# Attention scores of a macaron block: two of four query tiles computed as whole tiles, the last tile with its sides exchanged

## The chip, the cores and the metric

The kernel runs on one core of a Trainium2 chip. The core has a matrix engine (TensorE, "PE" in the profile, with its weight loads as "PEld"), a vector engine (VectorE, "DVE"), a scalar engine (ScalarE, "ACT"), a general engine (GpSimd, "POOL") and a queue that issues transfers (SyncE, "SP"). The metric is the device time of one execution in microseconds; lower is better. Everything is float32.

## The reference

A block of three parts is applied to `x` of shape (16, 512, 256): half a feed-forward part, attention, half a feed-forward part again, each added to `x`. The change touches attention alone:

```python
q = x @ Wq + bq                                   # x: the normalized input, (16, 512, 256)
k, v = jnp.split(x @ Wkv + bkv, [H * DQK], axis=-1)
q, k = _rope(heads(q)), _rope(heads(k))           # 16 heads of 64
scores = jnp.einsum('bhqd,bhkd->bhqk', q, k) * (1.0 / np.sqrt(DQK))
scores = jnp.where(causal, scores, -jnp.inf)      # a query sees keys up to its own place
probs = jax.nn.softmax(scores, axis=-1)
out = jnp.einsum('bhqk,bhkd->bhqd', probs, v)
return out.reshape(b, s, H * DV) @ Wo + bo
```

## The kernel before

Attention is worked off in 64 units, one for each batch (16) and group of four heads (4). A unit has 512 queries in four tiles of 128, numbered 0 to 3; by causality tile `i` needs `(i+1)*128` keys. The order of PE, DVE, ACT, POOL and SP in attention is written out by hand in the loop over `u` (from -2 to 63): each engine does its instructions in the order in which that loop gives them.

**Scores** (`Weights.scores`, L1038 to L1058). A head's 64 dimensions lie as two halves of 32 (the two parts of the rotation), the four heads of a unit in four groups of 32 rows. So a score matmul contracts 32 rows, is done for `n` = 0, 1 and accumulated, and the four heads stand beside each other in the four row groups of the array; each head has a PSUM bank of its own (`banks[j]`). Each tile is split into two halves of 64 queries, which stand on the two halves of the array's columns. The 64 early queries of a tile need 64 keys fewer than the late ones, so one half streams `w - 64` columns and the other `w`. Which half of the columns has the early queries alternates with the tile: in tiles 3 and 1 the first half, in tiles 2 and 0 the second. The 64 columns that the early half doesn't write are filled with zeros by a small bf16 matmul of a blank tile (L1047). Tiles 3 and 2 have four banks each (`scores((3,))`, `scores((2,))`); tiles 1 and 0 share four (`scores((1, 0))`).

An f32 matmul shows in the trace as two records of PE, each with a weight load of its own.

**Softmax** (`exps`, L1061 to L1079). For each head and tile DVE adds the causal mask, scales and takes the smallest (L1073), and ACT takes the exponential with its sum (L1077). `mask(i)` (L905) picks blocks of 128 columns out of one constant, `causal`, of 128 x 640, which POOL fills once. Since the sides alternate, there are two diagonal masks: one in the last block, for tiles with an even number, and one in block 3, for the odd ones.

**Weights onto values.** The weights are divided by their sums on POOL (L1085), turned in squares of 32 on DVE (L1100) and moved by SP (L1127). `sums` (L1149 to L1170) multiplies them with the values into `p_av` (L1158), and ACT copies the result out (L1169), adds the bias, and puts the queries of tiles whose sides are exchanged back in order: one copy for the odd tiles, two for the even ones. `leave` (L1171) multiplies with `Wo` into `p_ay` (L1176) and DVE adds it onto `x` (L1182).

**Order.** In a middle iteration PE does: `p_av` of unit `u`, scores of tiles 3 and 2 of unit `u+2`, `p_ay` of `u`, queries and keys of `u+3` (`p_q`, `p_k`, L988), values of `u+1` (`p_v`, L1010), scores of tiles 1 and 0 of `u+2`. PSUM has 8 banks in rotation: `p_ay` takes the bank that the scores of tile 3, head 0, had, and `p_av` those of the two key halves.

## Time and profile before

| | |
|---|---|
| median of 3 runs | 2297.73 us (2296.9 to 2299.47) |
| the profiled execution's own time | 2299.21 us |
| its span | 2297.5 us |
| attention, by the scores' first and last record | 410 to 1888 us of the span |
| score passes (L1054) | 8192, 303.4 us in which at least one runs |
| blank passes (L1047) | 1024 |
| distance of one attention unit from the next, in the middle | 23.26 us |
| granted clock of TensorE | 1.00 in the stretches shown below |

How to read what is shown below: in a group's line stand the line of the code, engine, operation, the tiles written and read, shapes and count, then the time in which at least one of them ran and the mean of one in ns, then the idle time of the engine just before them and who ended it. `32*64` in front of a matmul's shape is the part of the array that it uses, rows by columns. In the view by order of time a line has the start in us from the span's start, the length in us, and then the same; equal neighbours are put together, and records of two kinds that run side by side alternate, so that the shape is that of the first. Matmuls are pipelined: the end of a record is modelled, and the starts of two neighbours are the better measure. In the table of stretches each engine has its busy time and, in brackets, its number of instructions. In the waits stand who waited, for whom, the total in us, how often, and the longest.

### The profile page before, as it was taken

The page shows a single profiled execution, that of the slowest core. Times are in us where ns is not written, and L with a number is a line of the kernel's source. Part 1 is how long each engine was busy: PE and PEld are TensorE (multiplying, and loading weights), DVE is VectorE, ACT ScalarE, POOL GpSimd, SP SyncE. Part 2 cuts the span into 40 slices and gives each one's busy share as a digit, 9 for nine tenths or more (in the row PEclk, how much of TensorE's full clock was granted, in tenths as well). Part 3 has the DMA queues.
Part 4 walks back from the last instruction along what each step waited for, and adds up shares of the span by engine and source line. Part 5 has one row for each costly group of instructions (what it writes and reads, how often), then busy time and mean ns, then how long its engine had stood idle before and what let it go on. Part 6 is the DMA issues. An engine that isn't in the chain of part 4 may idle for free. (4 is left out here: it accounts for less than half of the span.)

```text
span 2297.5 us, 52884 instructions
## 1 busy us (share of the span) xinstructions
PE 2242.8 (98%) x19544; PEld 1486.4 (65%) x19544; DVE 1764.4 (77%) x4678; ACT 1158.7 (50%) x3296; POOL 1068.9 (47%) x1695
## 2 busy tenths in 40 slices
PE   7999999999999999999999999999999999998999
PEld 4664488566666666666666666666666666764588
DVE  6742298789989898989898989989888875432387
ACT  5743243555555555556465546555555565532233
POOL 2210053565566566565655565656556552210053
PEclk9999999999999999999999999999999999999999
DMA  6839851044545364454554554536455443839834
GB/s 223 251 123 404 334 141 56 12 129 122 141 116 159 100 157 125 127 136 113 146 133 126 131 144 108 159 96 162 120 132 131 124 117 113 239 137 406 309 118 139
DMA packets 221929, 359.52 MB, mean 156 GB/s; under 512 B 99876, under 2 KB 159848, under 8 KB 213480
## 3 DMA queue, kind: packets, MB, share of 16 engines
q1 hardware_dynamic: 220812, 355.34, 52.4%
q8 instruction: 155, 2.54, 0.5%
q14 instruction: 102, 0.84, 0.1%
q10 hardware_dynamic: 860, 0.81, 0.1%
HBM read 156.29 MB, written 37.22 MB: 84 GB/s over the span
## 5 line engine op out<-in xcount | busy, mean ns | idle before, releaser
L1085 POOL TENSOR_SCALAR pr<-pr,ars 128x512 f32<-128x512 f32 (+3 forms) x1024 | 524.1, 532 | 566.7 <-DVE ars L1082 565.5
L1077 ACT ACTIVATE pr<-pr,amn 128x512 f32<-128x512 f32 (+3 forms) x1024 | 561.8, 550 | 211.5 <-DVE amn L1073 207.1
L1100 DVE STREAM_TRANSPOSE sq<-pr 128x768 f32<-128x768 f32 x434 | 384.6, 918 | 79.6 <-DMA prT<-sq 56.8
L1073 DVE CUSTOM_DVE_ANT_0 pr<-p_as,causal 128x512 f32<-128x512 f32 (+2 forms) x768 | 309.4, 459 | 46.3 <-PE p_as L1054 46.1
L1054 PE MATMUL p_as<-k,q 32*64 32x448 f32 (+3 forms) x8192 | 303.4, 412 | 0.0
L1013 ACT COPY v<-p_v 128x512 f32<-128x512 f32 x128 | 74.8, 586 | 449.9 <-PE p_v L1010 449.9
L1158 PE MATMUL p_av<-prT,v 128*64 128x512 f32 (+3 forms) x2048 | 289.8, 435 | 9.3 <-ACT pr L1077 1.6
L1158 PEld LDWEIGHTS p_av<-prT,v 128*64 128x64 f32 x2048 | 160.3, 137 | 138.0 <-issue 93.1
L1176 PE MATMUL p_ay<-wo,aoT 128*128 128x256 f32 x1024 | 238.5, 386 | 0.8 <-ACT aoT L1169 0.5
L1054 PEld LDWEIGHTS p_as<-k,q 32*64 32x64 f32 x8192 | 206.6, 131 | 46.1 <-issue 23.7
L1010 PE MATMUL p_v<-wv,ahT 128*128 128x256 f32 x1024 | 231.6, 379 | 0.7 <-DVE x L1182 0.7
L988 PE MATMUL p_q<-ahT,wq 128*128 128x512 f32 x512 | 230.6, 593 | 0.2 <-ACT ahT L949 0.2
L988 PE MATMUL p_k<-ahT,wk 128*128 128x512 f32 x512 | 230.3, 592 | 0.0
L1010 PEld LDWEIGHTS p_v<-wv,ahT 128*128 128x128 f32 x1024 | 194.5, 190 | 53.8 <-issue 23.2
L1176 PEld LDWEIGHTS p_ay<-wo,aoT 128*128 128x128 f32 x1024 | 189.1, 190 | 55.8 <-DVE amn L1073 31.7
L1077 ACT ACTIVATION_READ_ACCUMULATOR pr<-pr,amn 128x1 f32 x1024 | 192.1, 188 | 0.0
L988 PEld LDWEIGHTS p_k<-ahT,wk 128*128 128x128 f32 x512 | 97.3, 190 | 122.0 <-issue 106.9
L988 PEld LDWEIGHTS p_q<-ahT,wq 128*128 128x128 f32 x512 | 97.0, 190 | 95.7 <-issue 78.4
L1073 DVE CUSTOM_DVE_ANT_1 pr<-p_as,causal 128x384 f32<-128x384 f32 x256 | 130.2, 546 | 0.0
L1169 ACT ACTIVATE aoT<-p_av,bcol 128x128 f32<-128x128 f32 (+1 forms) x384 | 117.4, 392 | 7.8 <-PE p_av L1158 7.8
L811 PE MATMUL p_cy<-vw,catT 128*128 128x256 f32 x512 | 120.8, 379 | 0.0
L584 PE MATMUL p_ds<-hT,qk 128*128 128x512 f32 x256 | 116.2, 597 | 2.1 <-ACT hT L159 2.1
(179 smaller groups left out, 3353.7 us busy)
## 6 DMA issues: line engine op xcount, KB each, us to landing
prT<-sq SPq DMA_DIRECT2D x992, 160.0 KB
w<-in_e_W_dram SPq DMA_DIRECT2D x64, 1024.0 KB
w<-in_e_Wg_dram SPq DMA_DIRECT2D x32, 1024.0 KB
out_dram<-x SPq DMA_DIRECT2D x64, 256.0 KB
awaya<-sqa SPq DMA_DIRECT2D x25, 512.0 KB
atT<-awaya SPq DMA_DIRECT2D x100, 128.0 KB
xl<-in_attn_x_dram SPq DMA_DIRECT2D x16, 512.0 KB
xl<-out_dram SPq DMA_DIRECT2D x16, 512.0 KB
```

Source lines behind the costliest of these rows:

```text
L584: nc.tensor.matmul(psc, qk[:, k, c * P:(c + 1) * P], hT[:, k, :], start=(k == 0), stop=(k == NC - 1))
L811: nc.tensor.matmul(py[:, t * D:(t + 1) * D], atT[:, c, t * P:(t + 1) * P], vws[b][:, c, :], start=(c == 0), stop=(c == NC - 1))
L988: nc.tensor.matmul(pq, self.w[:, k, at:at + P], hTs[self.b][:, k, :], start=(k == 0), stop=(k == NC - 1))
L1010: nc.tensor.matmul(pv[:, t * 256:(t + 1) * 256], hTs[b][:, k, (t0 + t) * P:(t0 + t + 1) * P], wv[:, k, hg * HG * DQ:(hg + 1) * HG * DQ], s ...
L1054: nc.tensor.matmul(banks[j][half * H:(half + 1) * H, at:at + wh], q[n][rows, q0:q0 + H], k[n][rows, :wh], start=(n == 0), stop=(n == 1))
L1073: nc.vector.tensor_tensor_reduce(out=by_block(self.at(i, j)), in0=by_block(banks[j][:, at:at + w]), in1=mask(i), scale=-1.0 / math.sqrt(DQ ...
L1077: nc.scalar.activation(self.at(i, j), self.at(i, j), AF.Exp, bias=self.mn[:, i, j:j + 1], scale=-1.0, accum_out=self.rs[:, i, j:j + 1])
L1085: nc.gpsimd.tensor_scalar(self.at(i, j), self.at(i, j), self.rs[:, i, j:j + 1], 1.0, ALU.mult, ALU.mult)
L1100: nc.vector.transpose(view(self.sq, j * blocks * SQ + dst[0] * SQ, [(blocks * SQ, nh)] + [(s * SQ, n) for s, (_, n) in zip(dst[1:], of)] + ...
L1158: nc.tensor.matmul(po[j * DQ:(j + 1) * DQ, :].rearrange("d (a f) -> d a f", a=NSQ)[:, :, t * SQ:], vs[u][:, t, head * DQ:(head + 1) * DQ], ...
L1169: nc.scalar.activation(dst[:, odd, to], src[:, odd, of], AF.Identity, bias=bcol[:, r:r + 1])
L1176: nc.tensor.matmul(py[:, t * D:(t + 1) * D], oTs[u][:, pair, (t0 + t) * P:(t0 + t + 1) * P], wo[:, hg * (HG // 2) + pair, :], start=(pair ...
```

## The change

Tiles 1 and 0 have all 128 queries on the whole width of the array: one matmul of `w` columns for each head and `n`, without blanks. Tiles 3 and 2 stay in halves (`by_halves`), but their sides are exchanged: tile 3 has its late queries on the first half, tile 2 its early ones. So only tile 3 has its queries out of order, and the mask, the constant behind it and the copies of L1169 follow: one copy for tiles 0 to 2 of 384 columns, two of 64 columns for tile 3, in place of one of 256 and two of 128.

```diff
-        nc.gpsimd.affine_select(out=causal[:, :S], in_=causal[:, :S], compare_op=ALU.is_ge, fill=NEG, base=S - P,
-                                pattern=[[-1, S]], channel_multiplier=1)
+        nc.gpsimd.affine_select(out=causal[:, S:], in_=causal[:, S:], compare_op=ALU.is_ge, fill=NEG, base=0,
+                                pattern=[[-1, P]], channel_multiplier=1)
         for half in range(2):
-            part = causal[half * H:(half + 1) * H, S:]
+            part = causal[half * H:(half + 1) * H, S - P:S]
...
-            return by_block(causal)[:, NT - i * 2:NT + 1:2] if i % 2 == 0 else by_block(causal)[:, NT - 1 - i:NT]
+            return by_block(causal)[:, :NT] if i == NT - 1 else by_block(causal)[:, NT - i * 2:NT + 1:2]
...
                 for i in tiles:
                     w = (i + 1) * P
-                    early = slice((i + 1) % 2 * H, ((i + 1) % 2 + 1) * H)
-                    for j in range(HG):
-                        zero = blank[j * 32:(j + 1) * 32, :]
-                        nc.tensor.matmul(banks[j][early, at + w - H:at + w], zero, zero, start=True, stop=True)
-                    for n in range(2):
-                        for j in range(HG):
-                            rows = slice(j * 32, (j + 1) * 32)
-                            for half in range(2):
-                                late = half ^ (1 - i % 2)
...
+                    if i < NT // 2:
+                        for n in range(2):
+                            for j in range(HG):
+                                rows = slice(j * 32, (j + 1) * 32)
+                                nc.tensor.matmul(banks[j][:, at:at + w], q[n][rows, i * P:(i + 1) * P],
+                                                 k[n][rows, :w], start=(n == 0), stop=(n == 1))
+                    else:
+                        self.by_halves(i, q, k, banks, at)
...
+            def by_halves(self, i, q, k, banks, at):
+                w, turned = (i + 1) * P, int(i == NT - 1)
+                early = slice(turned * H, (turned + 1) * H)
+                for j in range(HG):
+                    zero = blank[j * 32:(j + 1) * 32, :]
+                    nc.tensor.matmul(banks[j][early, at + w - H:at + w], zero, zero, start=True, stop=True)
+                for n in range(2):
+                    for j in range(HG):
+                        rows = slice(j * 32, (j + 1) * 32)
+                        for half in range(2):
+                            late = half ^ turned
+                            q0, wh = i * P + late * H, w - (1 - late) * H
+                            nc.tensor.matmul(banks[j][half * H:(half + 1) * H, at:at + wh],
+                                             q[n][rows, q0:q0 + H], k[n][rows, :wh],
+                                             start=(n == 0), stop=(n == 1))
...
-            dst = oTs[u][:, pair, :].rearrange("d (i o a y) -> d o a i y", i=NT // 2, o=2, a=NSQ)
-            src = po.rearrange("d (a i o y) -> d o a i y", i=NT // 2, o=2, a=NSQ)
-            for odd, to, of in ((1, slice(0, 4), slice(0, 4)), (0, slice(2, 4), slice(0, 2)),
-                                (0, slice(0, 2), slice(2, 4))):
-                nc.scalar.activation(dst[:, odd, to], src[:, odd, of], AF.Identity, bias=bcol[:, r:r + 1])
+            dst = oTs[u][:, pair, :].rearrange("d (i a y) -> d a i y", i=NT, a=NSQ)
+            src = po.rearrange("d (a i y) -> d a i y", i=NT, a=NSQ)
+            last = slice(NT - 1, NT)
+            for to, of, tiles in ((slice(0, 4), slice(0, 4), slice(0, NT - 1)), (slice(2, 4), slice(0, 2), last),
+                                  (slice(0, 2), slice(2, 4), last)):
+                nc.scalar.activation(dst[:, to, tiles], src[:, of, tiles], AF.Identity, bias=bcol[:, r:r + 1])
```

The order of the instructions on DVE, ACT, POOL and SP is the same as before; only the shapes named above differ. On PE the scores of tiles 1 and 0 have 16 matmuls in a unit where they had 32 and 8 blank ones; the rest stands where it stood.

More of the change, by code (lines that the diff above doesn't have):

```diff
@@ L1043, in scores @@
                     w = (i + 1) * P
-                    early = slice((i + 1) % 2 * H, ((i + 1) % 2 + 1) * H)
-                    for j in range(HG):
-                        zero = blank[j * 32:(j + 1) * 32, :]
-                        nc.tensor.matmul(banks[j][early, at + w - H:at + w], zero, zero, start=True, stop=True)
-                    for n in range(2):
-                        for j in range(HG):
-                            rows = slice(j * 32, (j + 1) * 32)
-                            for half in range(2):
-                                late = half ^ (1 - i % 2)
-                                q0, wh = i * P + late * H, w - (1 - late) * H
-                                nc.tensor.matmul(banks[j][half * H:(half + 1) * H, at:at + wh],
-                                                 q[n][rows, q0:q0 + H], k[n][rows, :wh],
-                                                 start=(n == 0), stop=(n == 1))
+                    if i < NT // 2:
[6 more added lines that the diff above has]
+                        self.by_halves(i, q, k, banks, at)
                     places.append((i, at))
```

## The prediction

> **What bounds the kernel now.** I read four views in this order: the shares of busy time, the table of busy time in stretches of one attention unit, the order in time of that unit, and the waits. The profiled execution took 2299.21 us, 1.71 more than its span of 2297.5; the three runs shown have a median of 2297.73, so what I work out on the profiled execution is lowered by 1.48 to compare it with the median.

> ```profile
> PE 2242.8 (98%) x19544; PEld 1486.4 (65%) x19544; DVE 1764.4 (77%) x4678; ACT 1158.7 (50%) x3296; POOL 1068.9 (47%) x1695
> ```

> 98% on PE is an average and says nothing on who waits for whom. The change lies in attention, from 410 to about 1912 us: 64 units (a batch and four heads), all but the first two and the last with the same period, 23.26 us in the middle. Here is one of them in four stretches: scores of tiles 1 and 0; p_av; scores of tiles 3 and 2; then p_ay, q, k and v.

> ```profile
> core 0: us, PE busy (x) PEld busy (x) DVE busy (x) ACT busy (x) POOL busy (x), PEclk, DMA share, GB/s
> 1004.86:1006.72 1.86, 1.75 (x73) 1.44 (x73) 1.13 (x2) 0.59 (x1) 1.86 (x3) 1.00 1.02 367
> 1006.72:1011.18 4.46, 4.46 (x32) 2.49 (x32) 4.35 (x21) 4.09 (x18) 4.04 (x9) 1.00 0.33 57
> 1011.18:1014.25 3.07, 3.07 (x74) 1.85 (x73) 3.07 (x6) 1.27 (x5) 1.49 (x4) 1.00 0.14 21
> 1014.25:1028.22 13.97, 13.97 (x52) 9.04 (x48) 12.14 (x31) 6.03 (x17) 9.65 (x12) 1.00 0.75 196
> ```

> In the second and third stretch DVE is as full as PE (4.35 of 4.46, 3.07 of 3.07). The order in time shows how the two are tied:

> ```profile
> 1004.96 0.22 PE L1047 MATMUL p_as<-blank 32*64 32x64 bf16 x4
> 1004.98 1.17 PE L1054 MATMUL p_as<-k,q 32*64 32x256 f32 x39
> ...
> 1006.56 0.42 DVE L1073 CUSTOM_DVE_ANT_0 pr<-p_as,causal 128x256 f32<-128x256 f32 x1 [0.31 <-PE p_as L1054]
> 1006.73 4.53 PE L1158 MATMUL p_av<-prT,v 128*64 128x512 f32 x32
> ...
> 1011.18 0.22 PE L1047 MATMUL p_as<-blank 32*64 32x64 bf16 x4
> ...
> 1013.53 0.65 DVE L1073 CUSTOM_DVE_ANT_0 pr<-p_as,causal 128x512 f32<-128x512 f32 x1
> ...
> 1014.25 2.42 PE L1176 MATMUL p_ay<-wo,aoT 128*128 128x256 f32 x10
> ```

> ```profile
> PEld p_ay L1176 <- DVE amn L1073: 31.7, 62, 0.9
> PEld p_av L1158 <- issue: 93.1, 364, 0.5
> DVE pr L1073 <- PE p_as L1054: 46.1, 57, 1.7
> ```

> DVE stands idle (0.31 us here, 57 times) until the first bank of tiles 1 and 0 is signalled, at 1006.541, and starts at 1006.564. Its list of masks, reciprocals and turns then runs to 1014.207, where it frees the bank that p_ay needs; p_ay's load starts 42 ns later and its first pass at 1014.251. That is the wait of p_ay on DVE, 62 times. So the loop of one unit is: the last v pass starts at 1004.648; 1.916 us to DVE's start; 7.687 to p_ay; 13.661 of back to back passes to the next unit's last v pass; 23.264 in all. PE's own road, scores of 1 and 0, p_av, scores of 3 and 2, is a second way to the same point: its last pass (started 1013.876, 427 long) ends at 1014.303, and a new kind of tile starts 70 ns before such an end wherever nothing else holds it, so PE could have begun p_ay at 1014.233, 18 ns before it did. DVE decides, PE is close behind.

> **The change, part by part.** A pass below is one record of a matmul: an f32 matmul is two.

> *Tiles 1 and 0 whole.* Per unit, 32 score matmuls and 8 blank ones become 16: PE loses 64−32+8 = 40 passes and 40 loads. The columns go the other way: a half of the array streamed 192+128 or 256+64 = 320 columns in each of its 4 passes, the whole array streams 256+128 = 384. At 216 ns a pass of 256 (the distance of p_v's passes), 64 columns cost 54 ns, four times 0.21 us. Yet today's group isn't bound by its columns. Its row group 0 starts passes of 192 at 1005.010, .202, .365, .527, then passes of 128 at .690, .811, 1006.085 and .242: the third waits 274 ns where 107 would do, since its weights are loaded only at 1006.081. From the first blank (1004.957) to that last start are 1285 ns.

> After: the same drain of 309 ns from the last v pass. Then the first load can't hide: after a change of tile kind p_ay's first pass of 256 is 483 long against 379, so 104 ns. Then 4 × 216 for tile 1, and three steps of tile 0 to its last start. A step with 128 columns and a 128-column load is 112 ns in p_cs, 109 in the transposes:

> ```profile
> L780 PE MATMUL p_cs<-kbd,cq 128*128 128x128 f32 x256 | 33.7, 275 | 0.7 <-POOL kbd L758 0.7
> ```

> (33.7 us for 256 is 32 runs of 8 × 112 plus the end of each.) So 104 + 864 + 3 × 109 to 112 = 1295 to 1304, 10 to 19 later than now. The pass of 128 in a 32-row tile ends 267 after its start as before. The signal follows today 32 ns after that end, because the other half stands behind it; where the bank's last write also ends last (tile 2: end 1014.263, signal 1014.277) it is 14, so 18 are won back. Net −8 to +1 ns on DVE's start; I take −3: 62 units × −0.003 = −0.2 us. The price is from rows, but no row has a tile of 32 rows and 128 columns. Bounds: if the first load hid behind the drain, −104 × 62 = −6.4 us. Nothing could go at the drain itself: p_z (128 rows) to p_bcol (62 rows, same columns) at 69.0 us also starts 69 ns before the modelled end. If a pass cost its load's whole 192 ns instead of 112, 3 × 80 = +0.24 us, 62 times +14.9 us.

> [...]

> *p_av.* It starts 383 ns after the last score pass where drain alone gives 197. In front of its load PE's sequencer works off five double waits:

> ```profile
> L1158 PEldq EVENT_SEMAPHORE  x310: 51/51/4237, 470.2 to 1902.7; - x155
> ```

> Five a unit, 105 ns apart, from 1006.190 to 1006.669; the load follows at 1006.694. They stand behind the last score matmul, which is issued late today. With 64 entries instead of 144 they can be worked off under the passes: p_av gets up to 186 ns earlier, plus some 40 since the last row group's last pass moves from 1006.342 to about 1006.30. Cover: none needed, as p_ay waits for DVE anyway. This gain of up to 0.23 us goes into p_ay's wait; it is worth nothing, and up to 14.0 us (62 × 0.226) if that wait were not there. On the other side it pays for any loss in tiles 3 and 2.

> What is next: the scores of 3 and 2 would begin up to 0.23 earlier; their banks come from DVE (heads 0 and 1 of tiles 1 and 0, done by 1007.8) and, for tile 2's blanks, from ACT's second aoT group, done 1012.457, with tile 2's first pass then due at 1012.54. No wait that reaches p_ay at 1014.25.

> *Tiles 3 and 2.* The same widths change sides: each half still has 448+384 or 512+320 = 832 columns a pass set, 8 blanks stay. Issue order within a pair turns round, and the half that is ahead now comes second in it. I take 0; a stall of up to 0.2 us is under the gain of p_av.

> *Masks.* Tile 1's mask turns from one stretch of 256 into two blocks; tile 2's has always had three.

> ```profile
> L1073 DVE CUSTOM_DVE_ANT_0 pr<-p_as,causal 128x512 f32<-128x512 f32 x224 | 141.9, 669 | 0.0
> L1073 DVE CUSTOM_DVE_ANT_1 pr<-p_as,causal 128x384 f32<-128x384 f32 x224 | 114.0, 546 | 0.0
> L1073 DVE CUSTOM_DVE_ANT_0 pr<-p_as,causal 128x256 f32<-128x256 f32 x224 | 94.2, 420 | 39.7 <-PE p_as L1054 39.6
> ```

> The split 384 lies 1.5 ns above the middle of 420 and 669 (544.5). Four in a unit, +6 ns at most, +0.4 us; since the reciprocal behind them waits for ACT (114 ns), I take one of the four, +0.1.

> *ACT's aoT copies.* 256+128+128 elements become 384+64+64. Starts lie 356 and 250 apart for 256 and 128, so 106 for 128: 462 + 197 + 197 = 856, as now. If 64 cost as much as 128, +0.21 us a unit on ACT, tile 2's blanks at 1012.67, still under p_ay's wait.

> *Setup and waits.* One causal fill shrinks from 512 to 128 columns, on a POOL that then stands idle until the first q at 401.8. The waits on DVE that stood on the blanks stand on the first four whole passes; what is queued behind them is the same, and those banks are free long before.

> *Sum:* 2299.21 − 0.2 + 0.1 = 2299.1; less 1.48: **2297.6 us**.

> **Rivals.**
> *Slower: 128-column loads of a 32-row tile are not hidden.* For it: no such tile in the trace, and the load record is 192 ns against 131 for 64 columns. Against: p_cs, and four row groups loading at once today (their first passes take effect within 20 ns). DVE's start has no slack, so it decides from the first nanosecond: +14.9, 2312.5; at half the exposure 2305.
> *Faster: PE's road decides after all.* If p_ay only seems to wait for DVE, p_av's 0.226 us comes through: −14.0, 2283.6. Against it: in 11 units p_av came 28 to 182 ns late, and only there did p_ay stand at drain's distance (357 ns) from the last score pass; in the others it follows DVE's signal by 42 ns. A smaller kind is the first load hidden in the drain, −6.4, 2291.2.
> *Slower: the turned sides make tile 2 stall by more than PE's new slack,* for instance each of its four passes by 64 columns, 0.21, and its blank, 0.06: 0.05 over the cover, +3 us, 2300.7, still inside what counts as no change.

> **How the numbers follow.** A difference of 0.2%, 4.6 us or 74 ns a unit, is about what a measurement of this kernel tells from no change. No change 0.70; loads exposed 0.18, most of it above 2302.3; a way to be faster 0.12, half of it the hidden first load. The forecast's own range is 2294 to 2301. To leave out no more than 2 in 10 it takes in the hidden first load below and the half exposed load above: 2291 to 2306.

> **What would show it.** Right: period 23.26 us; DVE starts 1.91 us after the last v pass; p_av about 0.2 us after the last score pass, and p_ay's wait for DVE grown to 0.2 us; 16984 matmul records. Wrong: steps of tile 0 far from 110 ns, a DVE start that moved by over 70 ns, or p_ay no longer behind DVE.

## The result, and the profile after

The changed kernel takes 2305.46 us (median of 15 runs, 2302.01 to 2308.77); the kernel before, in as many runs beside it, 2300.52 (2296.9 to 2304.16). The ratio is 1.0021, 95% interval 1.0013 to 1.0029: slower by about 0.2%, some 5 us. The prediction was no change. The profiled execution took 2307.27 us with a span of 2305.5.

Busy time first, then one attention unit in the same four stretches as before: scores of tiles 1 and 0; p_av; scores of tiles 3 and 2; p_ay, q, k and v.

```profile
PE 2260.8 (98%) x16984; PEld 1469.8 (64%) x16984; DVE 1764.4 (77%) x4678; ACT 1158.0 (50%) x3296; POOL 1068.5 (46%) x1695
```

```profile
core 0: us, PE busy (x) PEld busy (x) DVE busy (x) ACT busy (x) POOL busy (x), PEclk, DMA share, GB/s
1009.46:1010.98 1.52, 1.52 (x33) 1.35 (x32) 0.92 (x1) 0.58 (x1) 1.52 (x2) 1.00 0.99 348
1010.98:1015.44 4.46, 4.46 (x36) 2.14 (x33) 4.26 (x21) 3.84 (x17) 4.06 (x8) 1.00 0.40 65
1015.44:1018.84 3.40, 3.40 (x74) 1.98 (x72) 3.40 (x7) 1.55 (x7) 1.62 (x4) 1.00 0.02 2
1018.84:1032.81 13.97, 13.97 (x49) 9.04 (x48) 12.36 (x32) 5.98 (x17) 9.74 (x12) 1.00 0.79 198
```

PE has 2560 records fewer and is busy 18 us longer. From its first record (1004.96, 0.10 us behind the start of that row's window) the first stretch went from 1.77 to 1.52 us, as hoped, p_av and the last stretch didn't move, and the third grew from 3.07 to 3.40, with no more in it than before: 64 score passes and 8 blanks. Where, PE's order in time shows, of the kernel before first (from its first score pass to the last):

```profile
1011.20 2.07 PE L1054 MATMUL p_as<-k,q 32*64 32x512 f32 x36
1012.97 0.21 PE L1047 MATMUL p_as<-blank 32*64 32x64 bf16 x3
1013.00 0.46 PE L1054 MATMUL p_as<-k,q 32*64 32x320 f32 x1
1013.01 0.19 PE L1047 MATMUL p_as<-blank 32*64 32x64 bf16 x1
1013.01 1.29 PE L1054 MATMUL p_as<-k,q 32*64 32x320 f32 x27
```

The same of the changed kernel:

```profile
1015.45 2.12 PE L1070 MATMUL p_as<-k,q 32*64 32x512 f32 x35
1017.22 0.21 PE L1063 MATMUL p_as<-blank 32*64 32x64 bf16 x3
...
1017.26 1.65 PE L1070 MATMUL p_as<-k,q 32*64 32x320 f32 x28
```

Tile 3 has 32 passes. Ahead of tile 2's blanks there stood 36, that is four more: the first pass of tile 2's late half (384 columns) for each of the four heads. Now there are 35: one head is missing. In the single records heads 0, 1 and 2 start at 1017.027, .030 and .042, head 3 only at 1017.416, and it stays one pass behind the others to the end: their last late passes start by 1018.055, its own at 1018.432. The group of these passes says the same over the whole run (with its count, the time in which at least one ran, and the mean), first before, then after:

```profile
L1054 PE MATMUL p_as<-k,q 32*64 32x384 f32 x1024 | 94.2, 481 | 0.0
```

```profile
L1070 PE MATMUL p_as<-k,q 32*64 32x384 f32 x1024 | 121.7, 497 | 0.0
```

As many passes of nearly the same length, but at least one runs for 27.5 us longer, 0.43 us a unit: they lie beside each other less well.

The order in time of all engines, at the end of the same stretch:

```profile
1018.61 0.08 DVE L1086 DVE_READ_ACCUMULATOR2_ANT amn<- 128x1 f32 x1
...
1018.84 0.19 PEld L1190 LDWEIGHTS p_ay<-wo,aoT 128*128 128x128 f32 x1 [0.60 <-DVE amn L1086]
```

The last line names DVE as the one that p_ay's load waited for. That is out of date: DVE's read ends at 1018.69, 0.15 us ahead of p_ay, where before it ended 0.05 ahead (1014.20 and 1014.25). The name only says whose semaphore came last. p_ay now stands 411 ns behind head 3's last pass in every middle unit, that is 70 ns ahead of that pass's modelled end, which the prediction took for the distance where nothing but the pass holds it. And the passes of p_ay have next to no idle time in front of them (last number, in us over the whole run; e1 below has 11.8):

```profile
L1190 PE MATMUL p_ay<-wo,aoT 128*128 128x256 f32 x1024 | 238.6, 386 | 0.1
```

So PE decides, and the period is 23.350 us in all middle units, where its median was 23.262.

### The profile page after: what moved, and what is told of

Same layout as the page of the kernel before. It is cut to its first block, busy times and chain, and to the rows that moved or that the text cites. A ratio compares the mean times of both kernels' runs of the same rounds, so it can differ in the third digit from the quotient of the medians.

```text
span 2305.5 us, 47763 instructions
## 1 busy us (share of the span) xinstructions
PE 2260.8 (98%) x16984; PEld 1469.8 (64%) x16984; DVE 1764.4 (77%) x4678; ACT 1158.0 (50%) x3296; POOL 1068.5 (46%) x1695
## 5 line engine op out<-in xcount | busy, mean ns | idle before, releaser
L1086 DVE CUSTOM_DVE_ANT_1 pr<-p_as,causal 128x384 f32<-128x384 f32 (+1 forms) x512 | 237.7, 483 | 49.5 <-PE p_as L1048 49.4
L1086 DVE CUSTOM_DVE_ANT_0 pr<-p_as,causal 128x512 f32<-128x512 f32 (+1 forms) x512 | 235.1, 477 | 2.7 <-PE p_as L1070 2.7
L1171 PEld LDWEIGHTS p_av<-prT,v 128*64 128x64 f32 x2048 | 137.2, 137 | 146.6 <-issue 107.5
L1070 PE MATMUL p_as<-k,q 32*64 32x448 f32 (+3 forms) x4096 | 222.7, 520 | 0.0
L1070 PEld LDWEIGHTS p_as<-k,q 32*64 32x64 f32 x4096 | 116.5, 132 | 37.7 <-issue 25.2
L1183 ACT ACTIVATE aoT<-p_av,bcol 128x64 f32<-128x64 f32 (+1 forms) x384 | 117.1, 391 | 7.5 <-PE p_av L1171 7.5
```

Source lines behind the costliest of these rows:

```text
L1070: nc.tensor.matmul(banks[j][half * H:(half + 1) * H, at:at + wh], q[n][rows, q0:q0 + H], k[n][rows, :wh], start=(n == 0), stop=(n == 1))
L1086: nc.vector.tensor_tensor_reduce(out=by_block(self.at(i, j)), in0=by_block(banks[j][:, at:at + w]), in1=mask(i), scale=-1.0 / math.sqrt(DQ ...
L1171: nc.tensor.matmul(po[j * DQ:(j + 1) * DQ, :].rearrange("d (a f) -> d a f", a=NSQ)[:, :, t * SQ:], vs[u][:, t, head * DQ:(head + 1) * DQ], ...
L1183: nc.scalar.activation(dst[:, to, tiles], src[:, of, tiles], AF.Identity, bias=bcol[:, r:r + 1])
```

## The experiments

A kernel with more blanks (e7, e8, e10, e11) writes the same zeros twice. "Late half" is tile 2's half of 384 columns, "early half" its half of 320.

**e1: the order within a pair turned back.**

```diff
# the changed kernel
-                        for half in range(2):
+                        for half in (1, 0):
```

> The changed kernel with one thing turned: in tiles 3 and 2 each pair of halves issues the second half of the columns first, so that the half that is ahead is again the first of its pair, as in the kernel before. Theory (order and queue): in the changed kernel head 3's late half of tile 2 is issued 36 loads and matmuls after tile 2 begins and, with the last 28 of tile 3, has to wait until the first 512-column pass of tile 3's second round has ended; with the order turned it stands in front of that limit. Expected: scores of tiles 3 and 2 from 2.99 back to 2.69 us first to last pass, p_av still 0.20 us after the last whole-tile pass, p_ay again 42 ns behind DVE's signal, period 23.35 to 23.26 us, 62 times 0.09 = 5.5 us less than the changed kernel: about 2299 to 2300, 0.998 to 1.000 of before. Rival (the exchanged sides as such cost, whatever the order): 2.99 us and 1.002 stay. Rival (ACT's copies come too late for tile 2's blanks): 2.99 stays as well.

Measured: 2299.58 us (11 runs), ratio to before 0.9990 (0.9982 to 0.9999; before on that chip 2301.93 in 21 runs). The 36 are back:

```profile
1013.94 2.12 PE L1071 MATMUL p_as<-k,q 32*64 32x512 f32 x36
...
1015.75 1.29 PE L1071 MATMUL p_as<-k,q 32*64 32x320 f32 x27
1017.24 0.70 PE L1191 MATMUL p_ay<-wo,aoT 128*128 128x256 f32 x2 [0.19 <-DVE amn L1087]
```

```profile
PE p_ay L1191 <- DVE amn L1087: 11.8, 61, 0.2
```

The sides are as in the changed kernel, and so are ACT's copies, which tile 2's blanks wait for, and the stall is gone. So neither the sides nor the copies make it by themselves. Tiles 3 and 2 take 2.693 us from their first record to the last score pass (before 2.693, changed 2.991), the period is 23.262. And the array itself, not only its weight load, now stands idle 61 times for 0.19 us in front of p_ay until DVE is done: that is p_av's gain, and it leaves the period where it was. The 0.1% by which e1 is faster than the kernel before isn't in the period; in the two traces 60 units take 0.7 us less, since 11 of them came late before and none does in e1, and the rest of the 2.4 us stays open.

**e4: the sides alone.** The kernel before with tiles 3 and 2 exchanged and tiles 1 and 0 in halves as they were (mask and copies follow).

```diff
# the kernel before
-                    early = slice((i + 1) % 2 * H, ((i + 1) % 2 + 1) * H)
+                    turned = int(i % 3 == 0)
+                    early = slice(turned * H, (turned + 1) * H)
...
-                                late = half ^ (1 - i % 2)
+                                late = half ^ turned
```

> The kernel before with the sides of tiles 3 and 2 exchanged and nothing else: tiles 1 and 0 stay in halves with their sides as they were, masks and copies follow. Theory: the same stall, now without p_av's gain: scores of tiles 3 and 2 2.99 us, p_av 0.38 us behind the last pass of tiles 1 and 0, p_ay 0.41 us behind the last score pass; period 23.26 + 0.35 - 0.02 = 23.59, 62 times 0.335 = 20.8 us more than before: about 2321, 1.009. Rival (the loss came with the whole tiles 1 and 0): 2.69 us, 1.000.

Measured: 2319.59 us (4 runs), ratio 1.0077 (1.0064 to 1.0091), 17.7 us where 20.8 were expected; tiles 3 and 2 take 2.990 us and the period is 23.597, as expected to some ns. Again 35 passes ahead of the blanks:

```profile
995.49 2.07 PE L1056 MATMUL p_as<-k,q 32*64 32x512 f32 x35
```

So the loss is made by this part alone, and whole tiles 1 and 0 cover most of it.

**e3: tile 2's four blanks behind its scores,** the order of halves as in the changed kernel.

```diff
+                def blanks():
+                    for j in range(HG):
+                        zero = blank[j * 32:(j + 1) * 32, :]
+                        nc.tensor.matmul(banks[j][early, at + w - H:at + w], zero, zero, start=True, stop=True)
+                if turned:
+                    blanks()
...
+                if not turned:
+                    blanks()
```

> The changed kernel, its order of halves kept; only tile 2's four blank matmuls are issued behind its score matmuls and no longer ahead of them. Theory (queue of 64): head 3's late half then stands 28 and not 36 entries behind tile 2's start, so that it needs only tile 3's first round to have ended, which it has long: scores of tiles 3 and 2 at 2.69 to 2.75 us, period 23.26, about 2299 to 2300, 0.998 to 1.000 of before. Rival (turned sides or the order as such): 2.99 us, 1.002. Rival (ACT): the wait for ACT only moves from the blanks to the first score matmuls of heads 2 and 3, 2.99 us, 1.002.

Measured: 2302.35 us (11 runs), ratio 1.0004 (0.9994 to 1.0014). The four heads start within 28 ns and the last score pass starts 2.628 us after the first record, 65 ns earlier than in the kernel before; the 2.898 to the last record are the blanks, which now stand at the end, so the figure that was expected for both was wrong. The period is 23.263, p_ay behind DVE, so for the period neither the sides nor the order within a pair need to be touched. In time it is no faster than the kernel before, where 0.998 to 1.000 was expected; why e1 with the same period measured 2.8 us less isn't shown.

What e1 and e3 share is a smaller number of entries in PE's order between tile 3's 512-column passes and the load that stalled (56 in both, by the count that follows). Count two entries (load and pass) for each record: a blank has 2, a score matmul 4. Ahead of head 3's late load in the changed kernel stand 36 entries of tile 2 (8 of blanks, 8 for each of heads 0 to 2, 4 of its own early half), and 28 of tile 3 behind head 0's 512-column passes of the second set: 64 in all, so the entry just in front of the load is 64 places behind the last of these passes. That pass starts at 1016.793, is 587 long and ends at 1017.380; the load follows at 1017.412. With the other order the 512-column passes stand second in their pair and the late load first, 32 entries in: 64 places ahead of its pass lies a 448-column pass that has ended (in the kernel before, which has that order, at 1012.550, where head 3's pass starts at 1012.790). The next runs test this count.

**e6 and e9: one and two of the four blanks behind the scores** (head 3's; heads 2's and 3's).

> The changed kernel with one of tile 2's four blanks, that of head 3, issued behind the scores; the three others stay in front, the order of halves stays as changed. My theory (PE's queue takes 64 entries, so a load can enter only when the entry 64 places before it has finished, in order; the late head 3's load waits for the end of tile 3's second 512-column pass because 8 blank entries and 28 others of tile 2 stand between): with two entries fewer the same load has to wait only for the pass before, which ended 0.43 us earlier, so the whole stall goes, not a quarter of it. All four heads of tile 2's late half start within 40 ns of each other; last score pass at about 2.6 to 2.7 us after the first record of tiles 3 and 2 (2.85 to 2.90 with the one blank at the end), period 23.26 us. Rival (the blanks or the sides themselves cost, each head its share): head 3 still starts some 0.3 us behind the others, period above 23.30.

> The changed kernel with the blanks of heads 2 and 3 of tile 2 behind its scores, four queue entries fewer in front (with one moved, head 3's load came in time and its pass still waited for the end of tile 3's first 512-column pass of the second set). Count of 64 entries: the pass has now 62 entries between itself and that one and needs only what ended 0.43 us before, so all four heads of tile 2's late half start within 40 ns and no pass of the late half runs behind the others; with the two blanks at the end tiles 3 and 2 take 2.85 to 2.90 us, period 23.26. If half of the blanks meant half of the stall, head 3 would start about 0.2 us behind.

**e7, e8, e10, e11: e1's harmless order, with more blanks in front:** all four twice, those of heads 0 to 2 twice, head 3's twice, head 0's twice.

```diff
# e1; the list is that of e11
-                for j in range(HG):
+                for j in list(range(HG)) + ([] if turned else [0]):
                     zero = blank[j * 32:(j + 1) * 32, :]
```

> The changed kernel with the half that is ahead first in its pair (which had no stall), but with tile 2's four blanks written twice: 8 queue entries more. My theory: head 3's load of tile 2's late half now stands 40 entries into tile 2 and waits for the end of tile 3's last-but-three 512-column pass, the first of its second set: head 3 starts 0.35 to 0.40 us after heads 0 to 2, tiles 3 and 2 take 2.95 to 3.02 us from first to last pass where they took 2.69, and the period goes from 23.26 to about 23.35. Rival (the order within the pair or the sides, not the number of entries, made the stall): all four heads start together, four small blanks add under 0.1 us, period 23.26.

> The same with only heads 0 to 2's blanks written twice, 6 entries more. My theory with 64 entries: head 3's load then has to wait only for the 512-column pass before, which ended 0.43 us earlier, so there is no stall: four heads within some 40 ns, 2.69 to 2.78 us for tiles 3 and 2, period 23.26. Rival (blanks cost by their number): three quarters of what the kernel with four more shows.

> The changed kernel with the short half first in its pair, and one blank more in tile 2, that of head 3 written twice. Count of 64 entries: 66 would be needed for a stall, so none. A second limit that the run with three blanks more suggests, some six entries waiting for one tile (row group and half of the columns), which stops everything behind: head 3's own entries are the last of the round, nothing behind them is due soon: no stall either. Four heads within 40 ns, 2.69 to 2.72 us, period 23.26.

> The same with the one blank more given to head 0. Count of 64 entries alone: the same as with head 3's, no stall. The second limit (six waiting entries of one tile): head 0's early half then has seven entries waiting until its first blank starts, and with them stand heads 1, 2 and 3 of the late half: head 0 starts on time, the three others about 0.2 us later, right behind the start of the first blank; tiles 3 and 2 take 2.80 to 2.92 us, the period stays at 23.26 since 0.2 us lie under DVE.

Each of these kernels was timed once (e6 2298.66 beside 2298.22 for the kernel before; e9 2300.59, e10 2302.22 and e11 2301.36 beside 2305.71; e7 2309.69 and e8 2301.44 beside 2298.22), so the traces decide, and the times alone show nothing. Starts of the late half's first passes from the single records, in us after the stretch's first record:

| | entries of blanks in front | heads 0 / 1 / 2 / 3 | first record to last score pass | median period |
|---|---|---|---|---|
| changed | 8 | 1.586 / 1.589 / 1.601 / **1.975** | 2.991 | 23.350 |
| e4 | 8 | 1.586 / 1.589 / 1.601 / **1.974** | 2.990 | 23.597 |
| e6 | 6 | 1.587 / 1.590 / 1.602 / **1.967** | 2.932 | 23.290 |
| e9 | 4 | 1.585 / 1.589 / 1.600 / 1.614 | 2.660 | 23.270 |
| e3 | 0 | 1.586 / 1.589 / 1.601 / 1.614 | 2.628 | 23.263 |
| e1 (other order) | 8 | 1.586 / 1.589 / 1.594 / 1.607 | 2.693 | 23.262 |
| e10 | 10 | 1.586 / 1.589 / 1.594 / **1.771** | 2.803 | 23.270 |
| e11 | 10 | 1.586 / **1.793 / 1.807 / 1.820** | 2.838 | 23.264 |
| e8 | 14 | 1.585 / **1.793 / 1.806 / 1.998** | 2.963 | 23.323 |
| e7 | 16 | 1.586 / **1.794 / 1.807 / 2.007** | 3.024 | 23.382 |

e6 was expected to lose the whole stall and kept it: the expectation counted head 3's load and forgot that its pass stands one entry behind. The load came in time, 1.566 after the stretch's start, the pass, 64 places behind, at 1.967, 28 ns after the end of the same 512-column pass (1.939). e9, one blank further, lost the stall of that pass. So one entry decides, not the work in the blanks: from 8 to 6 only 8 ns of head 3's delay go, from 6 to 4 all the rest. e9 even shows the limit one pass on: there head 3's second late pass is the entry 64 places behind, and it starts at 1.965, 27 ns after the end of that same 512-column pass, 0.35 us after its first pass, where heads 0 to 2 take 0.32; p_ay's wait for DVE hides this. In the order in time, e6 first, then e9:

```profile
1011.18 2.07 PE L1074 MATMUL p_as<-k,q 32*64 32x512 f32 x35
...
1014.09 0.48 PE L1074 MATMUL p_as<-k,q 32*64 32x384 f32 x1
```

```profile
989.20 2.09 PE L1074 MATMUL p_as<-k,q 32*64 32x512 f32 x36
...
992.50 0.48 PE L1196 MATMUL p_ay<-wo,aoT 128*128 128x256 f32 x1 [0.23 <-DVE amn L1092]
```

In e6 one 384-column pass is left over behind everything else, and PE goes on to p_ay without idle time; in e9 PE waits 0.23 us for DVE.

e10 was a miss of the same kind: no stall was expected, head 3 came 0.16 us late. The entry 64 ahead of its pass is head 0's 448-column pass of tile 3, which starts at 1.210 and is 534 long: its end at 1.744 plus 27 ns is 1.771. The count holds; the expectation left out when that pass ends.

e8, expected without a stall, has two. Head 3's pass there stands 64 places behind a 512-column pass, again one entry more than its load. But head 1's stall the count doesn't allow, neither in e8 nor in e7: it isn't the only rule. e11 was made for this and came as its second theory said: one blank more for head 0 delays not head 0 but heads 1, 2 and 3, by 0.2 us, until 6 ns after the first blank starts (1.787). The line shows it; of the four late passes only one is ahead of the blanks:

```profile
990.09 2.07 PE L1071 MATMUL p_as<-k,q 32*64 32x512 f32 x33
991.86 0.19 PE L1064 MATMUL p_as<-blank 32*64 32x64 bf16 x1
991.87 0.53 PE L1071 MATMUL p_as<-k,q 32*64 32x384 f32 x1
```

Head 3's pass in e8 and its load in e7 come 53 and 58 ns after the end of head 0's 512-column pass (1.945), the one that the count names, where 28 and 32 were seen in e6 and the changed kernel. Why some 25 more stays open, and so does the exact number of the second limit: "some six waiting entries of one tile" fits e7, e8 and e11, but was tried at one place alone.

**e5: is DVE what is left?** e1 with two steps on DVE exchanged, so that the shorter turn (512 instead of 1024 columns) stands ahead of tile 3's mask, which p_ay waits for.

```diff
# e1
-                    old.turn_tile(1)
+                    old.turn_tile(0)
...
-                    old.turn_tile(0)
+                    old.turn_tile(1)
```

> The first experiment's kernel, and on DVE the turn of tile 0 (0.67 us) changes places with that of tile 1 (1.25 us), so that only the short one stands ahead of the mask of tile 3's first head, which frees p_ay's bank. Theory (DVE decides p_ay once the stall is gone, PE's road is 0.23 to 0.25 us ahead of it): the turn of tile 0 waits some 0.3 us for POOL, the bank is free about 0.18 us earlier, period 23.08, 62 times 0.18 = 11 us less than the first experiment: about 2288 to 2290, 0.995 of before; the second p_ay may then wait for its bank, which gives back up to 0.1 us a unit. Rival (PE decides): same time as the first experiment, 0.998 to 1.000.

Measured: 2292.96 us (5 runs), ratio 0.9963 (0.9951 to 0.9976): it beats both kernels, by less than expected. DVE waits for POOL in front of the turn that was moved forward (18.7 us, 62 times), 0.3 us each, as expected, and the median period is 23.100 where 23.08 was said. But the mean of the middle ones is 23.170: 12 of them take 23.23 to 24.03 us, and in single units DVE starts up to 1 us late. In the four longest a turn waits 1.2 to 2.7 us for the DMA transfers that move the turned weights:

```profile
DVE sq L1114 <- DMA prT<-sq: 60.1, 44, 2.7
```

e1 has nearly as much of these waits (55.8 us, 46 times) without such units; why they cost time here isn't shown.

## Why the prediction was wrong

**The loop, right.** DVE's start 1.915 us after the last v pass (said 1.91), p_av 0.200 us after the last score pass (said about 0.2), 16984 matmul records, a unit of 23.262 us when only the stall is taken away (e1). What it named as wrong if seen, p_ay no longer behind DVE, is what happened.

**Tiles 1 and 0 whole, right.** Head 0's passes take 1300 ns from the first start to the last, where 1295 to 1304 was said (all four heads 1320, before 1385); the steps of tile 0 are 109, 112 and 111 ns with loads of 185, and DVE starts within 2 ns of before. These loads of 128 columns in a tile of 32 rows are hidden; the rival that priced them at +14.9 us is out, and so is the hidden first load (−6.4).

**p_av, right.** PE reaches it 0.248 us earlier (65 ns from the scores of tiles 1 and 0, 183 from the waits; 0.226 was said), and e1 shows that it leaves the period as it was as long as DVE decides. That PE's road decides after all was the faster rival; e5 shows what it needs, a DVE that is earlier.

**Tiles 3 and 2, the step that failed:** "The same widths change sides [...] Issue order within a pair turns round, and the half that is ahead now comes second in it. I take 0; a stall of up to 0.2 us is under the gain of p_av." The sentence has the mechanism's seat, the order in which the half that is ahead is issued, but puts it at nothing, and gives no reason why a stall should stay under the 0.2 us that p_av covers. The runs show a stall in place of the 0: head 3's late load (in e6 its first pass) is held until tile 3's 512-column pass 64 entries ahead has ended. It cost 0.298 us up to the last pass, and 0.054 more because that pass is now one of 384 columns, 481 long, in place of one of 320, 427 long. The sum by the prediction's own terms: PE's road was 18 ns ahead of DVE's; −248 from p_av, +298 and +54 from tiles 3 and 2, so 86 ns behind DVE (88 in the period); 62 times that is 5.3 us. Measured are 4.9; in the kernel before some units came later than 23.262 for other reasons and now don't (60 distances between units sum to 1397.3 us before, 1401.9 after). That 2305.46 us lies within 2291 to 2306 is luck: the upper end stood there for half-exposed loads, which didn't come, and the kernel before, beside it, measured 2.8 us more than the median that the sum started from.

**The third rival** had the place and the effect, tile 2 stalling by more than PE's new slack, with 0.05 us over the cover where 0.086 came of the terms, and was filed under no change. But it had another mechanism: it priced the passes by their columns; how far ahead the late half's loads had to be issued wasn't asked. The trace of before had the answer: there, the load at 1006.081, which the prediction quotes as late, comes 31 ns after the end of a 256-column pass of tile 1 (1005.676 and 374 long, so 1006.050), which by the same count stands 64 places ahead of the entry in front of it. The prediction took it as a fact of that group and not as a rule.

**Masks and copies, right.** aoT's three copies start 462, 196 and 196 ns apart, 854 where 856 was said; from DVE's start to p_ay's load the median is 7.682 us in e1 and 7.681 before.

## What to carry to other kernels

When passes of several tiles run side by side at different speeds, order their instructions by when they become due: count the entries between a tile's first load and the passes still running (in the changed kernel the load 65 places behind such a pass was held, and its own pass came 0.37 us late), and let the half that is ahead be issued first in its pair. Here an edit that keeps every width made tiles 3 and 2 longer by 0.298 us by its order alone (2.991 us, and 2.693 in e1). And a gain that goes into a wait is cover only up to its size: price the term set against it from the trace, not at nothing.

## What the runs showed of the hardware

Within these 64 places a second, nearer limit showed: in e11 one blank more waiting for a tile of the array (head 0's early half) held back the late halves of heads 1 to 3, which are other tiles, until 6 ns after its first blank had started (head 1 at 1.793, the blank at 1.787); the same blank given to head 3 (e10) left heads 1 and 2 on time (1.589 and 1.594).
